# Eight one-bank PSUM tiles in one pool, and layer 0's attention in bursts of up to three half key tiles

## The chip, the cores and the metric

The kernel runs on one core of a Trainium2 chip. The metric is device time in microseconds (us) for one execution, which processes eight images. Five engines work side by side, each through its own instruction queue and in the order of that queue: TensorE (PE, with its weight loads listed as PEld), VectorE (DVE), ScalarE (ACT), GpSimd (POOL) and SyncE (SP, which here only issues DMAs).

## The reference

The input is eight images of 32x32 positions with 384 channels, in fp32. Layer 0 is attention with decomposed relative positions, layer 1 a causal attention followed, for a part of the batch, by an FFN with sign-binarized weights and quantized activations. Cut to what matters:

```python
# layer 0, per image: 6 heads of 64, 1024 positions
qkv = gn(x) @ qkv_w + qkv_b                     # gn: group norm, 32 groups
attn = (q * SCALE) @ k.T
attn += rel_h[:, :, :, :, None] + rel_w[:, :, :, None, :]   # q against row and column tables
x = x + softmax(attn) @ v @ proj_w + proj_b
# layer 1, per image: one head of 384, causal
t = ln(x); t = x + softmax(mask((t @ Wq) @ (t @ Wk).T * scale)) @ (t @ Wv)
# FFN: groups of the batch, NUM_GROUPS = 5, group size 8 // 5 = 1
h = quant(ln(t) @ sign(W1 - mean).T + b1)       # quant: scale by the group's absmax, clip
out = quant(gelu(h) @ sign(W2 - mean).T + b2)   # images beyond the five groups get zero
x = t + out
```

With eight images and five groups of one image each, only images 0 to 4 have an FFN, and its absmax runs over one image.

## The kernel before

The program goes through the images one after the other. For each image b it does the following, and PE's part of each is given with its line.

1. Query, key and value projections of layer 0. `queries_keys(m)` for m = 0, 1, 2 gives the queries of three head pairs (L368, through `project_T`), for m = 3, 4, 5 the keys (L435). After m = 1, 2, 3, `positions(p)` multiplies the queries by the position tables (L461), copies the result from PSUM into pages on ACT (L466) and DVE (L467), and sends it through DRAM (L473, L478) so that it comes back in the layout of scores. `place` splits it in a high and a low part (ACT L491, DVE L492) and puts it into the four tiles `r` by DMA (L499, half of them on SP's queue and half on POOL's). The values come last (L511).
2. Layer 0's attention (`attend0_fast`). For each of three head pairs p, eight key tiles c and two query halves, `scores` makes a half key tile for two heads: two products of queries and keys (L562) and two that add the positions from `r` by a 0/1 matrix (L566). These use row tiles of 64 of PE's rows, so that two heads run side by side. ACT then exponentiates both heads' scores in one instruction of 128x1024 (L571). `values` adds the exponentials up on DVE (L578) and multiplies by the values (L582), in column tiles of 64 columns. The loop makes the two halves of tile c, then the values of tile c - 1. At the first tile of the first pair, `residual` loads x and adds the projection's bias on POOL in one instruction (L545). For image 0 the same loop also calls `binarize` (L255, L256), which computes the FFN's signs on DVE.
3. Output projection (L671, L378), layer norm (`layer_norm_T`: statistics L340, root on ACT L344, normalized rows `xn` on DVE L357, transposes on PE L295, copies L350 and L351), queries of layer 1 (L741), values (L378), the statistics of the next image's group norm (L317, L324), causal attention (L781, L795).
4. For images 0 to 4 the FFN: a second layer norm in both halves, product y1 (L890) with its bias on ACT (L894) and absmax on DVE (L901), the absmax over all partitions (`absmax_scale`: DVE L851, POOL L853, DVE L854 to L857), two gelus of each part on ACT (L914, L915), product y2 (L929), a second absmax, a clip on POOL (L939) and the addition to x on DVE (L943). This last addition and the output DMA (L973) of image b are done within step 1 of image b + 1.

The order of the instructions on each engine is settled when the program is built: instructions are placed by the scheduler of the language's tile framework, and a tile of a pool takes over a buffer from an earlier tile of the same pool in the order in which the code asks for them. PSUM, of eight banks, is divided in two pools:

```python
self.ps_s = pool("ps_s", 2, space=PSUM)   # tiles of two banks: s_tile
self.ps_o = pool("ps_o", 4, space=PSUM)   # tiles of one bank: o_tile
```

`ps_s` holds layer 0's scores, layer 1's scores, the query projections (L368), the third pair's positions and the first output projections. `ps_o` holds all else: key and value projections, the other positions, accumulators, transposes, y1 and y2. In SBUF, `page` has 12 buffers of 128x1024, and `work` has two buffers for `xn`.

Of the kernel before, what the change touches and what calls it, by code (L numbers as in the profile page):

```python
# [9 lines left out]
F32 = mybir.dt.float32  # L10
# [22 lines left out]
MASKED = -3.0e38  # L33

# [4 lines left out]
class Pools:  # L39
    def __init__(self, ctx, tc, path):  # L40
        self.path, self.fast = path, path == "f"

        def pool(name, bufs, **kw):
            return ctx.enter_context(tc.tile_pool(name=f"{path}_{name}", bufs=bufs, **kw))

        self.image_ = pool("image", 11)
        self.page_ = pool("page", 12 if self.fast else 8)
        self.work = pool("work", 2)
        self.small = pool("small", 3)
        self.ps_s = pool("ps_s", 2, space=PSUM)  # L50
        self.ps_o = pool("ps_o", 4, space=PSUM)

    def s_tile(self, name):
        return self.ps_s.tile([P, 2, 512], F32, tag="s", name=f"{self.path}_{name}")
# [20 lines left out]
def conv_attn_hybrid(  # L75
# [42 lines left out]
    def load_weights(pools):  # L118

        nc.scalar.dma_start(out=bqk, in_=qkv_b[0 : 2 * C].rearrange("(m p) -> p m", p=P))  # L120
        nc.vector.memset(rel, 0.0)
        for half in range(2):
            nc.scalar.dma_start(out=rel[half * HD : (half + 1) * HD, 0, : 2 * H - 1], in_=rel_hT)
            nc.scalar.dma_start(out=rel[half * HD : (half + 1) * HD, 1, : 2 * W - 1], in_=rel_wT)
        nc.scalar.dma_start(out=bv, in_=qkv_b[2 * C : 3 * C].rearrange("(m p) -> p m", p=P))
        nc.scalar.dma_start(out=b1_sb, in_=b1.rearrange("(m p) -> p m", p=P))
        src = qkv_w.rearrange("(p k) o -> p k o", k=NC)
        for i in range(3):
            nc.sync.dma_start(out=wqkv_sb[:, :, ts(i, C)], in_=src[:, :, ts(i, C)])
        nc.sync.dma_start(out=wproj_sb, in_=proj_w.rearrange("(k p) o -> p k o", p=P))  # L130
        nc.sync.dma_start(out=pb, in_=proj_b.partition_broadcast(P))
        nc.sync.dma_start(out=wv_sb, in_=wv.rearrange("(k p) o -> p k o", p=P))
        nc.sync.dma_start(out=b2_sb, in_=b2.partition_broadcast(P))

        nc.scalar.mul(wqkv_sb[:, :, 0:C], wqkv_sb[:, :, 0:C], qscale)
        nc.scalar.mul(bqk[:, 0:NPAIR], bqk[:, 0:NPAIR], qscale)
        nc.scalar.mul(rel, rel, 1.0 / qscale)

# [77 lines left out]
    def binarize(pools):  # L216
# [30 lines left out]
        for which, w, dst, n_out, last in pieces("sign"):  # L247
            gs = n_out // NG
            step = min(C // gs, w.shape[1])
            for k in range(0, w.shape[1], step):  # L250
                for g in range(NG):
                    wg, m = w[:, k : min(k + step, w.shape[1]), ts(g, gs)], mean[:, which, g : g + 1]
                    above = pools.work.tile([P, C], F32, tag="xn", name=f"above_{which}_{n_out}")
# [34 lines left out]
    def stages(pools):  # L288
# [17 lines left out]
        def group_norm_T(b, xT=None):  # L306

            xT = load_T(b) if xT is None else xT
            st = pools.small.tile([P, NC, 2, 6], F32, tag="gst", name=f"gst_{b}")
# [24 lines left out]
        def layer_norm_T(xt, xT, half, name, xlo=None):  # L334
# [20 lines left out]
            for i, j in enumerate(js):  # L355
                xn = pools.work.tile([P, C], F32, tag="xn", name=f"xn_{name}_{j}")
# [5 lines left out]

        def project_T(w, cols, xT, name):

            ps = pools.s_tile(name)
            for k in range(NC):
                for half in range(2):
                    nc.tensor.matmul(  # L368
                        ps[:, half, :], w[:, k, cols], xT[:, k, ts(half, 512)],
                        start=(k == 0), stop=(k == NC - 1),  # L370
                    )
            return ps.rearrange("p a n -> p (a n)")
# [19 lines left out]
        def softmax_numerator(sc, n, total, name):  # L392

            nmax = pools.small.tile([P, 1], F32, tag="nmax", name=f"nmax_{name}")
            nc.vector.tensor_reduce(nmax, sc[:, :n], AX.X, ALU.max, negate=True)
            pr = pools.page(f"pr_{name}")
            nc.scalar.activation(pr[:, :n], sc[:, :n], AF.Exp, bias=nmax, accum_out=total)
            return pr
# [15 lines left out]
        def layer0(b, xT):  # L414
# [9 lines left out]
            def queries_keys(m):  # L424
                p = m % NPAIR
                bias = bqk[:, m : m + 1]
                both = project_T(wqkv_sb, ts(m, P), xT, f"qk_{b}_{m}") if m < NPAIR else None
                for half in range(2):
                    t = ts(half, 512)
                    if m < NPAIR:  # L430
                        dst, ps = q[:, p, t], both[:, t]
                    else:
                        ps = pools.o_tile(f"qk_{b}_{m}_{half}")
                        for i in range(NC):
                            nc.tensor.matmul(  # L435
                                ps, wqkv_sb[:, i, ts(m, P)], xT[:, i, t], start=(i == 0), stop=(i == NC - 1)
                            )
# [11 lines left out]
            def positions(p):  # L449
# [6 lines left out]
                for half in range(2):  # L456
                    ps = [pools.o_tile(f"rel_{b}_{p}_{half}_{par}") for par in range(2)] if p < NPAIR - 1 else (
                        pools.s_tile(f"rel_{b}_{p}_{half}").rearrange("i a n -> a i n")
                    )
# [83 lines left out]
            def residual():  # L543
                xt = load_x(pools, b)
                nc.gpsimd.tensor_tensor(xt, xt, pb.unsqueeze(1).to_broadcast([P, NJ, C]), ALU.add)  # L545
# [4 lines left out]
        def attend0_fast(residual, b, q, k, r, v, later):  # L550
# [7 lines left out]
            def scores(p, c, half):  # L558

                sc = pools.s_tile(f"s0_{b}_{p}_{c}_{half}")  # L560
                for par in range(2):
                    nc.tensor.matmul(  # L562
                        sc[:, par, :], k[rows[par], p, ts(c, P)], q[rows[par], p, ts(half, 512)], start=True, stop=False
                    )
                for par in range(2):
                    nc.tensor.matmul(  # L566
                        sc[:, par, :], unit[rows[par], c // 2 % 2].rearrange("i h w -> i (h w)"),
# [3 lines left out]
                last_exp[0] = nc.scalar.activation(pr, sc.rearrange("p a n -> p (a n)"), AF.Exp).ins  # L571
                return pr

            def values(p, c, prs, first, sums, avs):
                if c:
                    for half in range(2):
                        prev = first[half] if c == 1 else sums[half]
                        nc.vector.tensor_tensor(sums[half], prev, prs[half], ALU.add)  # L578
                for half in range(2):
                    for par in range(2):  # L580
                        h = 2 * p + par
                        nc.tensor.matmul(  # L582
                            avs[half][ts(par, HD), :], v[:, c, ts(h, HD)], prs[half][:, ts(par, 512)],
                            start=(c == 0), stop=(c == NJ - 1),
                        )

            def reciprocals(p, tot):

                rt = pools.small.tile([P, 32], F32, tag="rt0", name=f"rt0_{b}_{p}")
# [8 lines left out]
            def set_aside(p, sums, avs):  # L598
# [3 lines left out]
                few = pools.small.tile([P, 2, 2, 16], F32, tag="few", name=f"few_{b}_{p}")  # L602
# [34 lines left out]
            pending = []  # L637
            for p in range(NPAIR):
                sums = [pools.page(f"sum0_{b}_{p}_{half}") for half in range(2)]
                for c in range(NJ):  # L640
                    prs = [scores(p, c, half) for half in range(2)]
                    if c == 0:
                        first = prs
                    if pending:
                        values(*pending.pop())
                    if c == 0:
# [5 lines left out]
                    if b == 0 and xt is None and (c % 2 or p == NPAIR - 1) and next(signs[0]):  # L652
                        xt = residual()
                    if p == 0 and c > 0:
                        with tc.issue_after(last_exp[0]):
                            next(later, None)
                    if c == 3 and p > 0:
                        divide(p - 1, few)
                    pending.append((p, c, prs, first, sums, avs))
                last = (sums, avs)  # L660
            values(*pending.pop())
# [4 lines left out]
            for j in range(4):  # L666
                if j % 2 == 0:
                    both = pools.s_tile(f"pj_{b}_{j}")
                begun.append(both[:, j % 2, :C])
# [13 lines left out]
        def attend0_general(residual, b, q, k, r, v, later):  # L683
# [3 lines left out]
            def scores(u):  # L687
# [4 lines left out]
                sc = pools.s_tile(f"s0_{b}_{j}_{h}")  # L692
                rows = ts(par, HD)
                for half in range(2):
                    nc.tensor.matmul(
                        sc[:, half, :], q[rows, p, ts(j, P)], k[rows, p, ts(half, 512)], start=True, stop=False
                    )
                    for i in range(4):
                        nc.tensor.matmul(
                            sc[:, half, ts(i, P)], r[2 * half + i % 2][rows, p, ts(j, P)],  # L700
# [3 lines left out]
                    sc.rearrange("p a n -> p (a n)"), T, state["tot", j][:, h : h + 1], f"0_{b}_{j}_{h}"  # L704
# [65 lines left out]
        def attend1_fast(xt, b, q, xT, v):  # L770
# [5 lines left out]
            def scores(c):  # L776
                sc = pools.s_tile(f"s1_{b}_{c}")
                for half in range(c // 4, 2):
                    lo = max(0, c * P - half * 512)
                    for k in range(NC):  # L780
                        nc.tensor.matmul(  # L781
                            sc[:, half, lo:], xT[:, c // 4, k, ts(c % 4, P)], q[:, half, k, lo:],
                            start=(k == 0), stop=(k == NC - 1),
                        )
                sc = sc.rearrange("p a n -> p (a n)")
                nc.vector.tensor_tensor(sc[:, ts(c, P)], sc[:, ts(c, P)], maskT, ALU.add)  # L786
                at = sum(NJ - i for i in range(0 if c < 3 else 3, c)) * P
                pr = room[c >= 3][:, at : at + (NJ - c) * P]
                nc.scalar.activation(pr, sc[:, c * P :], AF.Exp)  # L789
# [26 lines left out]
        def attend1_general(xt, b, q, xT, v):  # L816
# [3 lines left out]
            def scores(j):  # L820
                n = (j + 1) * P
                sc = pools.s_tile(f"s1_{b}_{j}")
                for half in range((n + 511) // 512):
                    w = min(512, n - half * 512)
                    for k in range(NC):
                        nc.tensor.matmul(
                            sc[:, half, :w], q[:, j // 4, k, ts(j % 4, P)], xT[:, half, k, :w],
                            start=(k == 0), stop=(k == NC - 1),
                        )
                sc = sc.rearrange("p a n -> p (a n)")  # L830
                nc.vector.tensor_tensor(sc[:, ts(j, P)], sc[:, ts(j, P)], mask, ALU.add)
# [197 lines left out]
```

## Time and profile before

| | us |
|---|---|
| time, median of 3 runs | 2480.84 (2468.26 to 2485.35) |
| the profiled run | 2481.89, span 2480.1, mean granted TensorE clock 0.993 |
| PE busy | 2405.8 |
| DVE busy | 1430.6 |
| ACT busy | 992.7 |
| POOL busy | 231.9 |

The page of the profile lists instructions by source line, with the busy time of the group, the mean time of one, and how long the engine was idle just ahead of them. One image with an FFN takes about 331 us. Layer 0's attention takes about 101 us of an image (for image 6, from 2012.9 to 2113.9). Ends of matmuls are modelled in the profile and neighbouring ones overlap, so times on PE are best read from start to start.

### The profile page before, as it was taken

The page shows a single profiled execution, that of the slowest core. Times are in us where ns is not written, and L with a number is a line of the kernel's source. Part 1 is how long each engine was busy: PE and PEld are TensorE (multiplying, and loading weights), DVE is VectorE, ACT ScalarE, POOL GpSimd, SP SyncE. Part 2 cuts the span into 40 slices and gives each one's busy share as a digit, 9 for nine tenths or more (in the row PEclk, how much of TensorE's full clock was granted, in tenths as well). Part 3 has the DMA queues.
Part 4 walks back from the last instruction along what each step waited for, and adds up shares of the span by engine and source line. Part 5 has one row for each costly group of instructions (what it writes and reads, how often), then busy time and mean ns, then how long its engine had stood idle before and what let it go on. Part 6 is the DMA issues. An engine that isn't in the chain of part 4 may idle for free.

```text
span 2480.1 us, 25259 instructions
## 1 busy us (share of the span) xinstructions
PE 2405.8 (97%) x9378; PEld 1264.7 (51%) x9378; DVE 1430.6 (58%) x2182; ACT 992.7 (40%) x1323; POOL 231.9 (9%) x333
## 2 busy tenths in 40 slices
PE   7989999999999999999999999999999999999998
PEld 3435684345763356743558434566435543554344
DVE  3696554963466744658545486346674258524852
ACT  3441273631555414655127363155541155114520
POOL 0210002200013000030000220001300030002000
PEclk9999999999999999999999999999999999999999
DMA  7812207210054101181110621003500270017100
GB/s 158 246 52 102 77 1 161 68 64 31 8 103 127 51 13 38 28 189 40 39 38 1 161 68 64 8 31 86 143 26 1 68 156 32 1 43 158 30 0 27
DMA packets 154787, 169.92 MB, mean 69 GB/s; under 512 B 113408, under 2 KB 126048, under 8 KB 153120
## 3 DMA queue, kind: packets, MB, share of 16 engines
q1 hardware_dynamic: 134416, 98.93, 16.9%
q0 software_dynamic: 17184, 69.22, 9.2%
q8 instruction: 76, 1.25, 0.2%
q10 hardware_dynamic: 3056, 0.08, 0.1%
q14 instruction: 55, 0.45, 0.1%
HBM read 75.38 MB, written 42.47 MB: 48 GB/s over the span
## 4 chain that ended last, share of the span: by engine, by line
PE 93%; DVE 3%; ACT 2%; issue 1%; DMA 1%; POOL 0%; ACTq 0%; DVEq 0%; POOLq 0%
PE f_s L562 14%; PE f_av L582 14%; PE f_s L781 8%; PE f_av L795 8%; PE f_y L890 6%; PE f_y L929 6%; PE f_qk L435 5%; PE f_v L378 5%; PE f_v L511 5%; PE f_q L741 5%; PE f_qk L368 4%; PE f_s L566 3%; PE f_pj L378 3%; PE f_rel L461 2%; PE f_pj L671 2%; PE f_pt L295 1%
## 5 line engine op out<-in xcount | busy, mean ns | idle before, releaser
L571 ACT ACTIVATE f_pr<-f_s 128x1024 f32<-128x1024 f32 x384 | 390.5, 1025 | 380.9 <-PE f_s L566 343.0
L562 PE MATMUL f_s<-f_q,f_k 64*128 64x512 f32 x1536 | 414.2, 618 | 22.7 <-ACT f_pr L571 22.7
L578 DVE TENSOR_TENSOR f_sum<-f_sum,f_pr 128x1024 f32<-128x1024 f32 x288 | 337.6, 1220 | 97.5 <-ACT f_pr L571 97.0
L582 PE MATMUL f_av<-f_pr,f_v 128*64 128x512 f32 x1536 | 370.0, 604 | 0.0
L566 PE MATMUL f_s<-f_r,unit 64*128 64x512 f32 x768 | 297.6, 773 | 0.0
L562 PEld LDWEIGHTS f_s<-f_q,f_k 64*128 64x128 f32 x1536 | 132.1, 186 | 216.1 <-ACT f_pr L571 146.9
L582 PEld LDWEIGHTS f_av<-f_pr,f_v 128*64 128x64 f32 x1536 | 94.0, 136 | 219.3 <-issue 212.6
L781 PE MATMUL f_s<-f_q,f_lnT 128*128 128x512 f32 (+3 forms) x576 | 197.2, 488 | 0.0
L795 PE MATMUL f_av<-f_v,f_pr 128*128 128x385 f32 x576 | 194.5, 486 | 0.0
L492 DVE TENSOR_TENSOR f_far<-f_near,f_far 64x1024 fp32r<-64x1024 f32 x32 | 95.1, 2973 | 99.4 <-ACT f_far L491 85.1
L435 PE MATMUL f_qk<-f_gnT,wqkv_sb 128*128 128x512 f32 x288 | 135.4, 626 | 16.8 <-DVE f_far L467 16.8
L795 PEld LDWEIGHTS f_av<-f_v,f_pr 128*128 128x128 f32 x576 | 108.6, 190 | 78.6 <-issue 11.5
L499 POOL DMA_DIRECT2D f_r<-f_far x192 | 101.8, 532 | 446.8 <-DVE f_far L492 412.6
L781 PEld LDWEIGHTS f_s<-f_q,f_lnT 128*128 128x128 f32 x576 | 101.4, 190 | 73.9 <-issue 50.2
L368 PE MATMUL f_qk<-f_gnT,wqkv_sb 128*128 128x512 f32 x288 | 132.1, 601 | 3.0 <-DVE f_gnT L329 3.0
L894 ACT ACTIVATE f_h<-f_y,b_sb 128x256 f32<-128x256 f32 x240 | 100.8, 472 | 68.1 <-PE f_y L890 68.0
L901 DVE TENSOR_REDUCE am<-f_h 128x1 f32<-128x1024 f32 (+2 forms) x80 | 71.6, 947 | 97.7 <-ACT f_h L894 97.7
L741 PE MATMUL f_q<-f_lnT,wqk 128*128 128x512 f32 x288 | 127.5, 592 | 0.0
L378 PE MATMUL f_v<-wv_sb,f_lnT 128*128 128x384 f32 x384 | 126.5, 486 | 0.0
L511 PE MATMUL f_v<-wqkv_sb,f_gnT 128*128 128x384 f32 x384 | 125.1, 486 | 0.0
L566 PEld LDWEIGHTS f_s<-f_r,unit 64*128 64x128 f32 x768 | 74.2, 187 | 93.5 <-issue 93.5
L789 ACT ACTIVATE f_pr<-f_s 128x1024 f32<-128x1024 f32 (+3 forms) x64 | 41.7, 651 | 199.1 <-DVE f_s L786 199.1
(162 smaller groups left out, 3091.9 us busy)
## 6 DMA issues: line engine op xcount, KB each, us to landing
f_far<-f_far SPq DMA_DIRECT2D x48, 512.0 KB, 3.8
f_r<-f_far POOLq DMA_DIRECT2D x192, 128.0 KB, 3.5
f_r<-f_far SPq DMA_DIRECT2D x192, 128.0 KB, 3.3
f_gnT<-in_xT SPq DMA_DIRECT2D x24, 512.0 KB, 4.8
f_x<-in_x SPq DMA_DIRECT2D x32, 384.0 KB, 5.6
out_y<-f_x POOLq DMA_DIRECT2D x28, 384.0 KB, 3.8
f_near<-f_far SPq DMA_DIRECT2D x128, 64.0 KB, 4.3
f_w1a<-w1s POOLq DMA_DIRECT2D x5, 1536.0 KB, 6.9
```

Source lines behind the costliest of these rows:

```text
L368: nc.tensor.matmul(ps[:, half, :], w[:, k, cols], xT[:, k, ts(half, 512)], start=(k == 0), stop=(k == NC - 1),)
L378: nc.tensor.matmul(ps[:, :C], xT[:, k, ts(j, P)], w[:, k, cols], start=(k == 0), stop=(k == NC - 1))
L435: nc.tensor.matmul(ps, wqkv_sb[:, i, ts(m, P)], xT[:, i, t], start=(i == 0), stop=(i == NC - 1))
L511: nc.tensor.matmul(ps, keys[:, i, j // 2, j % 2], wqkv_sb[:, i, 2 * C :], start=(i == 0), stop=(i == NC - 1))
L562: nc.tensor.matmul(sc[:, par, :], k[rows[par], p, ts(c, P)], q[rows[par], p, ts(half, 512)], start=True, stop=False)
L566: nc.tensor.matmul(sc[:, par, :], unit[rows[par], c // 2 % 2].rearrange("i h w -> i (h w)"), r[2 * (c // 4) + c % 2][rows[par], p, ts(half ...
L571: last_exp[0] = nc.scalar.activation(pr, sc.rearrange("p a n -> p (a n)"), AF.Exp).ins
L578: nc.vector.tensor_tensor(sums[half], prev, prs[half], ALU.add)
L582: nc.tensor.matmul(avs[half][ts(par, HD), :], v[:, c, ts(h, HD)], prs[half][:, ts(par, 512)], start=(c == 0), stop=(c == NJ - 1),)
L741: nc.tensor.matmul(ps, wqk[:, k, ts(m, P)], xT[:, half, k, :], start=(k == 0), stop=(k == NC - 1))
L781: nc.tensor.matmul(sc[:, half, lo:], xT[:, c // 4, k, ts(c % 4, P)], q[:, half, k, lo:], start=(k == 0), stop=(k == NC - 1),)
L795: nc.tensor.matmul(av[:, : C + 1], prs[c][:, ts(j - c, P)], v[:, c, :], start=(c == 0), stop=(c == j))
```

## The change

PSUM becomes one pool, `ps_o`, of eight tiles of one bank. What was one tile of two banks becomes two tiles of one: scores of layer 0 (one per head), scores of layer 1 (one per 512 keys), query projections, positions, output projections. Instructions on them are divided likewise, so that an exp of 128x1024 becomes two of 128x512.

Layer 0's attention no longer alternates two half tiles of scores with the values of the tile before. The sixteen half tiles of a head pair are made in six bursts of 2, 3, 3, 3, 3 and 2; after each burst's scores come the values of the burst before. `values` works on one half tile. The calls of `residual`, `divide`, `binarize` and `place` follow the bursts.

The bias of the output projection is added to x in eight instructions of 384 columns. `xn` gets a pool of its own with three buffers (some small buffers go from three to two). A square root of a constant, `early_root`, is computed on ACT after the loads of the weights.

```diff
+BURSTS = (2, 3, 3, 3, 3, 2)
+BURSTS_AT = [sum(BURSTS[:i]) for i in range(len(BURSTS))]
...
+        self.xn = pool("xn", 3)
...
-        self.ps_s = pool("ps_s", 2, space=PSUM)
-        self.ps_o = pool("ps_o", 4, space=PSUM)
-
-    def s_tile(self, name):
-        return self.ps_s.tile([P, 2, 512], F32, tag="s", name=f"{self.path}_{name}")
+        self.ps_o = pool("ps_o", 8, space=PSUM)
...
+        early = pools.small.tile([P, 1], F32, tag="early", name="early_root")
+        nc.scalar.activation(early, ones[:, 0:1], AF.Sqrt)
...
-                xn = pools.work.tile([P, C], F32, tag="xn", name=f"xn_{name}_{j}")
+                xn = pools.xn.tile([P, C], F32, tag="xn", name=f"xn_{name}_{j}")
...
-                both = project_T(wqkv_sb, ts(m, P), xT, f"qk_{b}_{m}") if m < NPAIR else None
                 for half in range(2):
                     t = ts(half, 512)
+                    ps = pools.o_tile(f"qk_{b}_{m}_{half}")
+                    for i in range(NC):
+                        nc.tensor.matmul(
+                            ps, wqkv_sb[:, i, ts(m, P)], xT[:, i, t], start=(i == 0), stop=(i == NC - 1)
+                        )
...
-                nc.gpsimd.tensor_tensor(xt, xt, pb.unsqueeze(1).to_broadcast([P, NJ, C]), ALU.add)
+                for j in range(NJ):
+                    nc.gpsimd.tensor_tensor(xt[:, j, :], xt[:, j, :], pb, ALU.add)
...
-                sc = pools.s_tile(f"s0_{b}_{p}_{c}_{half}")
+                sc = [pools.o_tile(f"s0_{b}_{p}_{c}_{half}_{par}") for par in range(2)]
...
-                last_exp[0] = nc.scalar.activation(pr, sc.rearrange("p a n -> p (a n)"), AF.Exp).ins
+                for par in range(2):
+                    last_exp[0] = nc.scalar.activation(pr[:, ts(par, 512)], sc[par], AF.Exp).ins
...
-            pending = []
+            units = [(c, half) for c in range(NJ) for half in range(2)]
+            bursts = [units[at : at + n] for at, n in zip(BURSTS_AT, BURSTS)]
+            pending, first = [], [None, None]
             for p in range(NPAIR):
                 sums = [pools.page(f"sum0_{b}_{p}_{half}") for half in range(2)]
-                for c in range(NJ):
-                    prs = [scores(p, c, half) for half in range(2)]
-                    if c == 0:
-                        first = prs
-                    if pending:
-                        values(*pending.pop())
-                    if c == 0:
+                for n, burst in enumerate(bursts):
+                    prs = [scores(p, *u) for u in burst]
+                    for u in pending:
+                        values(*u)
+                    if n == 0:
...
-                    if b == 0 and xt is None and (c % 2 or p == NPAIR - 1) and next(signs[0]):
+                    if b == 0 and xt is None and next(signs[0]):
                         xt = residual()
-                    if p == 0 and c > 0:
+                    if p == 0 and n > 0:
                         with tc.issue_after(last_exp[0]):
                             next(later, None)
-                    if c == 3 and p > 0:
+                    if n == 2 and p > 0:
                         divide(p - 1, few)
-                    pending.append((p, c, prs, first, sums, avs))
+                    pending = [(p, *u, pr, sums, avs) for u, pr in zip(burst, prs)]
...
-                if j % 2 == 0:
-                    both = pools.s_tile(f"pj_{b}_{j}")
-                begun.append(both[:, j % 2, :C])
+                begun.append(pools.o_tile(f"pj_{b}_{j}")[:, :C])
...
                 for half in range(c // 4, 2):
+                    sc = pools.o_tile(f"s1_{b}_{c}_{half}")
```

## The prediction

> **What bounds the kernel now.** I read the page first: busy shares, then the chain that ended last.
>
> ```profile
> PE 2405.8 (97%) x9378; PEld 1264.7 (51%) x9378; DVE 1430.6 (58%) x2182; ACT 992.7 (40%) x1323; POOL 231.9 (9%) x333
> ...
> PE 93%; DVE 3%; ACT 2%; issue 1%; DMA 1%; POOL 0%; ACTq 0%; DVEq 0%; POOLq 0%
> ...
> L571 ACT ACTIVATE f_pr<-f_s 128x1024 f32<-128x1024 f32 x384 | 390.5, 1025 | 380.9 <-PE f_s L566 343.0
> ```
>
> TensorE (PE) is busy for 97% and carries 93% of the chain, so an edit pays only where PE loses time. I therefore added up, over all pairs of neighbouring PE records, what their start spacing has beyond its steady value: 160 of 2480 us. An fp32 matmul is two records (passes), 0.429 us apart at 512 columns; a pair of 64-row tiles shares a pass slot.
>
> The timeline of one stretch of layer 0's attention shows the steady cycle (start, length, engine, line).
>
> ```profile
> 2039.65 1.13 PE L562 MATMUL f_s<-f_q,f_k 64*128 64x512 f32 x4
> ...
> 2042.03 1.94 PE L582 MATMUL f_av<-f_pr,f_v 128*64 128x512 f32 x8
> 2043.89 1.13 PE L562 MATMUL f_s<-f_q,f_k 64*128 64x512 f32 x4
> ```
>
> A cycle of two half tiles takes 4.25 us (2043.89 to 2048.14 is the next). Scores take 2 x (2 x 0.429 + 0.234 for L566), values 4 x 0.429, together 3.9: PE loses 0.151 us from row-tiled scores to column-tiled values and 0.201 us back. The rest of the 160 us is in waits. In the timeline after the first FFN:
>
> ```profile
> 385.42 5.74 POOL L939 TENSOR_SCALAR f_y<-f_y,qu,ql 128x384 f32<-128x384 f32 x8 [7.15 <-PE f_rel L461]
> 386.10 1.02 DVE L943 SCALAR_TENSOR_TENSOR f_x<-f_y,qs,f_x 128x384 f32<-128x384 f32 x1 [1.75 <-POOL f_y L939]
> 387.16 1.91 DVE L467 COPY f_far<-f_rel 64x512 f32<-64x512 f32 x3
> 387.90 7.05 PE L435 MATMUL f_qk<-f_gnT,wqkv_sb 128*128 128x512 f32 x12 [3.15 <-DVE f_far L467]
> ```
>
> PE waits for a PSUM bank that VectorE (DVE) frees (L467), and DVE waits for GpSimd (POOL). Two more stretches show PE not waiting where it could: between the transposes of the second layer norm, and while the absmax between the FFN's products y1 and y2 goes DVE, POOL, DVE, ACT.
>
> ```profile
> 626.42 0.82 PE L295 MATMUL f_pt<-ident,xn 128*128 128x128 f32 x6
> ...
> 627.08 2.74 PE L368 MATMUL f_qk<-f_gnT,wqkv_sb 128*128 128x512 f32 x6
> ...
> 630.31 3.60 PE L368 MATMUL f_qk<-f_gnT,wqkv_sb 128*128 128x512 f32 x8
> ...
> 631.06 1.28 ACT L344 ACT_TABLE_LOAD   x1
> ...
> 634.40 1.02 PE L368 MATMUL f_qk<-f_gnT,wqkv_sb 128*128 128x512 f32 x2
> ...
> 635.83 0.48 PE L890 MATMUL f_y<-f_lnT,f_w1a 128*128 128x512 f32 x1
> ```
> ```profile
> 669.28 3.59 PE L368 MATMUL f_qk<-f_gnT,wqkv_sb 128*128 128x512 f32 x8
> ...
> 671.10 0.17 DVE L851 TENSOR_REDUCE qg<-am 128x1 f32<-128x16 f32 x1
> ...
> 672.46 0.61 ACT L914 ACTIVATE f_hi<-f_h,qs 128x384 fp32r<-128x384 f32 x1 [2.15 <-DVE qs L857]
> ...
> 673.13 0.79 PE L929 MATMUL f_y<-f_w2a,f_hi 128*128 128x384 f32 x3 [0.26 <-ACT f_hi L914]
> ```
>
> L368 there is the next image's query projection: 16 + 8 passes, 6.87 + 3.43 us of useful work in holes. It can be there because its PSUM tiles come from `ps_s`, which the FFN doesn't use.
>
> [...] L492 took 8.44 us beside the 6.73 us residual add L545. [...] Roughly: after spacing losses of 3.83 to 4.06 us passes took 0.425 us more for a while (1.1 to 2.6 us in all); after 3.14 and 3.15 us none did.
>
> **The change part by part.** The order of instructions in the two built programs was compared engine by engine.
>
> *Bursts.* Eighteen bursts replace 24 in each image. Counted in the programs, row-to-column changes fall from 182 to 136, column-to-row from 175 to 128: 46 x 0.151 + 47 x 0.201 = **-16.4 us**. They fit in the banks: six for three half tiles, two for the accumulators. The exp L571 becomes two of 128x512; nearest row is the ACT copy of that shape, 0.58 us. A cycle of three half tiles is 3 x 1.092 + 6 x 0.429 + 0.352 = 6.2 us of PE, six exps 3.5 us of ACT; the last ends about 3.28 + 1.16 = 4.4 us into the cycle, before PE needs the banks again: nothing, hidden beside PE. The DVE sums keep their number and size; `divide` and `place` come at other bursts, with r's DMAs landing over 10 us before their use.
>
> *Bank waits before the third projection.* With eight banks in rotation L435 takes others than L467 is freeing, and in the new DVE order most L943 come before these copies. The five stalls are 3.94, 3.15, 3.14, 4.06 and 3.83 us; less a 0.2 us mode change each, 17.1; the slow passes behind them 5.8; three other images lose 0.6 each: 17.1 + 5.8 + 1.8 = **-24.7 us**.
>
> *Attention start.* PE waits twice, 1.15 us each (18.4 us over eight images), for an exp. The new order puts four score pairs first (all eight banks), then waits for exp 0's two halves, and again later. From 0 to -18.4; the halves come some 0.3 us earlier at each: **-5 us**.
>
> *Residual add.* Eight POOL instructions of 384 columns (nearest L939, 0.7 us) for one of 6.75. PE hides it, except in image 0, [...] (two L256 took 7.4 us) and PE loses 8.88 us at 145. Binarizing is also called at every burst. Between 0 and -8.9: **-4.5 us**.
>
> *Norm buffers.* The first layer norm loses 1.45 us per image (11.6) on DVE's xn. A third buffer frees only the wait on the transposes, not DVE's own 0.43 us per tile: 0 to -8, taken **-3 us**. The square-root table is loaded (1.28 us, ACT at 13.46) before it is needed: **-1.3 us**.
>
> *What the single pool takes away.* In the new PE order the next image's first query projections stand after the last y2: 24 transposes, 144 y1, 192 y2 in one piece. Tiles of one pool take banks in the order of the code, so the projection can't overtake.
> Absmax: the chain is unchanged, the 3.43 us of work leave it: 5 x 3.43 = **+17.2 us** (15 to 18).
> Second layer norm: before, y1 began 9.41 us after the last attention product, 6.87 of it projection: 2.54 net. After, by DVE's new order: x7's update done at 1.3 us, three low parts (0.51 each) 2.8, fourth xn 3.2, statistics (0.56 + 0.18 + 0.17) 4.2. ACT's fourth cast ends at 4.4, then table load 1.28 and root: 5.9; reciprocal 6.2; four xn with a buffer wait 7.9; transposes, y1 at 8.55. Loss 6.0 x 5 images with an FFN = **+30 us** (25 to 33).
> One matmul (0.86) inside y2, where ACT paces PE anyway: 0 to 4.3, **+2 us**.
> gvar now follows gmean directly; two L781 passes stood between. At the start that wait was 0.96 us: 7 x 0.86 = **+6 us** (0 to 7).
> Clock: the absmax pause becomes 3.6 us, near the point where passes slow: 0 to 25, **+4 us**.
>
> Sum: gains 16.4 + 24.7 + 5 + 4.5 + 3 + 1.3 = 54.9; losses 17.2 + 30 + 2 + 6 + 4 = 59.2; net +4.3 on the profiled 2481.9: **2486 us**. That run is within 0.05% of the median 2480.84 (runs 2468.26 to 2485.35).
>
> **The rivals.**
> A, the sum as above, 2468 to 2504: 0.50. Within it a variant: r arrives late. Image 6, whose order resembles the new one, needed r part 0 44.4 us after its first L461 and had it after 37.4; image 1 took 42.5. Two us late on five images would give 2496.
> B, slower: the clock. If the 3.6 us pause after y1 and the two of 2.2 and 3.0 us in the layer norm lower it, y1 and y2 each begin with up to 2.6 us of slow passes: 5 x (2.6 + 2.6) less the 4 taken is +22: 2508. It decides once the pause passes what separates 3.15 (no slow pass) from 3.83 (slow). For: 3.6 is nearer the latter. Against: y2's start is paced by ACT (a gelu pair each 1.2 us for 0.5 us of matmul), which hides some. 0.28.
> C, faster: the waits collapse together. Attention starts lose nothing (-13.4 more), image 0's stall goes (-4.4), the first norm gains 8 (-5), the second norm costs 25 (-5), y2 and clock nothing (-6): -33.8, 2452. For: all are waits on a buffer or engine that the change relieves. Against: exp's own time stands. 0.22.
> That the bursts aren't made is excluded by the built order.
>
> **How the numbers follow.** About 1% is what a measurement of this kernel tells from no change: faster is below 2456, slower above 2506. The chances are those of C, A and B. The range runs from inside C to beyond B's point, 2455 to 2514, since the clock, image 0 and the attention start each reach some 5 to 20 us.
>
> **What would show it.** Right: three-unit cycles of about 6.2 us; no stall before L435; L943 off PE's way; PE idle about 3.6 us between y1 and y2 and some 5 us in the second layer norm, five times; the first y1 about 8.5 us after the last attention product; no query projection inside the FFN. Wrong: y1 starting within 5 us, attention cycles with exp waits, PE waiting for r at the first L566, or passes of 0.85 us after the pauses.

## The result, and the profile after

The changed kernel takes 2511.5 us (median; 2508.5 to 2514.4) against 2476.8 us for the kernel before in the same rounds (2468.3 to 2485.4): a ratio of 1.014, 95% interval 1.0099 to 1.0181. It is 1.4% slower. That lies inside the stated range, but it is the side to which 0.28 was given, not the likeliest case. The traced run before was 5 us slower than this median, the traced run after 3 us faster than its own, so the traces differ by 26.4 us and the medians by 34.7; in which stage the other 8 us lie, no trace shows.

The page of the changed kernel, with the lines that answer to those of before and one new group:

```profile
PE 2405.9 (96%) x9378; PEld 1296.8 (52%) x9378; DVE 1416.6 (57%) x2182; ACT 1016.2 (41%) x1742; POOL 300.4 (12%) x389
...
PE 93%; DVE 2%; DMA 2%; ACT 1%; POOL 1%; issue 1%; SPq 0%; ACTq 0%; DVEq 0%
...
L569 ACT ACTIVATE f_pr<-f_s 128x512 f32<-128x512 f32 x768 | 408.5, 597 | 351.5 <-PE f_s L563 294.3
...
L542 POOL TENSOR_TENSOR f_x<-f_x,pb 128x384 f32<-128x384 f32 x64 | 117.9, 1871 | 10.0 <-issue 9.7
```

PE's busy time is the same to 0.1 us while the span grew by 26.4 us, so the loss shows as PE's waiting. (Inside the busy time two things offset each other: fewer mode changes, that is, changes between row-tiled and column-tiled products, and the slow passes that are met below.) ACT pays 18 us for halving the exps, and nobody waits for that. POOL's residual add L542 takes 1.87 us for one of eight; the single instruction before took 6.75.

Both traces can be cut at PE's first instruction of each stage. Summed over the images, the stages differ as follows (after minus before, us of the profiled runs):

| stage of PE | difference |
|---|---|
| start to the first position product | -1.1 |
| first position product to the values (L457 to L507) | -20.6 |
| values and layer 0's attention | -8.3 |
| output projection and first layer norm | -6.1 |
| layer 1's queries to the end of its attention | +9.5 |
| end of attention to the next first position product: second norm, y1, y2, and now all of the moved projections | +53.5 |

Five times 0.86 us of projection went from the last stage to the second one, so the FFN's own loss is 57.8 and the second stage's own gain 24.9. The sum is 26.9, the rest of 0.5 lies at the end.

The second layer norm in the timeline after (image 1):

```profile
630.21 1.15 PE L296 MATMUL f_pt<-ident,xn 128*128 128x128 f32 x9
...
633.42 0.52 PE L296 MATMUL f_pt<-ident,xn 128*128 128x128 f32 x3 [2.06 <-DVE xn L358]
...
634.47 1.28 ACT L345 ACT_TABLE_LOAD   x1
...
636.22 1.26 DVE L358 TENSOR_SCALAR xn<-f_x,lmv,lrs 128x384 f32<-128x384 f32 x3
...
636.75 2.82 PE L296 MATMUL f_pt<-ident,xn 128*128 128x128 f32 x12 [2.81 <-DVE xn L358]
...
639.22 0.71 PE L890 MATMUL f_y<-f_lnT,f_w1a 128*128 128x512 f32 x1
```

PE stands idle for 2.06 and 2.81 us where the projection used to be. The last twelve transposes take 2.82 us where six took 0.82: their starts are 0.21 us apart, not 0.108. The clock is low there: the trace has a granted clock of 0.50 from 636.75 to 639.20, and 1.00 over the same stage before (626 to 636). The low clock reaches into y1: in the five images its first passes, one to eight of them, start 0.27 to 0.57 us apart in place of 0.23 (0.32 for the very first), 3.6 us more than before in all. Between y1 and y2 the bracket gives the pause and its releaser, and the projection follows only after y2:

```profile
672.76 0.40 PE L890 MATMUL f_y<-f_lnlo,f_wrest 128*128 128x512 f32 x1
676.83 0.97 PE L929 MATMUL f_y<-f_w2a,f_hi 128*128 128x384 f32 x3 [3.67 <-ACT f_hi L914]
677.98 1.33 PE L929 MATMUL f_y<-f_w2a,f_hi 128*128 128x384 f32 x3 [0.19 <-ACT f_hi L914]
```
```profile
712.08 10.46 PE L430 MATMUL f_qk<-f_gnT,wqkv_sb 128*128 128x512 f32 x24
722.47 1.99 PE L457 MATMUL f_rel<-f_q,rel 64*128 64x512 f32 x8
```

From the fifth pass of y2 on, seven starts lie 0.32 us apart where most lay 0.17 to 0.18 apart before. The clock records say the same: 0.50 from 677.3 to 680.7.

In layer 0's attention the bursts run as they were meant to, from 2060.78 to 2066.98 in 6.2 us (PE, image 6), but pair 1 meets a new wait:

```profile
2060.78 1.13 PE L559 MATMUL f_s<-f_q,f_k 64*128 64x512 f32 x4
...
2064.26 2.79 PE L580 MATMUL f_av<-f_pr,f_v 128*64 128x512 f32 x12
2066.98 1.13 PE L559 MATMUL f_s<-f_q,f_k 64*128 64x512 f32 x4
...
2074.29 0.50 PE L563 MATMUL f_s<-f_r,unit 64*128 64x512 f32 x2 [1.08 <-DMA f_r<-f_far]
```

The wait stands at the same place in images 1 to 7; only here does the profile name its releaser.

What holds that transfer shows in POOL's queue at the same time, where six additions stand ahead of the remaining issues for `r`:

```profile
2056.51 0.55 POOL L495 DMA_DIRECT2D f_r<-f_far  x1
2057.08 11.79 POOL L542 TENSOR_TENSOR f_x<-f_x,pb 128x384 f32<-128x384 f32 x6
2068.81 3.17 POOL L495 DMA_DIRECT2D f_r<-f_far  x6
```

### The profile page after: what moved, and what is told of

It is laid out like the page before. It is cut to its first block, busy times and chain, and to the rows that moved or that the text cites. A ratio compares the mean times of both kernels' runs of the same rounds, so it can differ in the third digit from the quotient of the medians.

```text
span 2506.5 us, 25716 instructions
## 1 busy us (share of the span) xinstructions
PE 2405.9 (96%) x9378; PEld 1296.8 (52%) x9378; DVE 1416.6 (57%) x2182; ACT 1016.2 (41%) x1742; POOL 300.4 (12%) x389
## 4 chain that ended last, share of the span: by engine, by line
PE 93%; DVE 2%; DMA 2%; ACT 1%; POOL 1%; issue 1%; SPq 0%; ACTq 0%; DVEq 0%
PE f_s L559 14%; PE f_av L580 14%; PE f_qk L430 10%; PE f_av L794 7%; PE f_s L781 7%; PE f_y L929 7%; PE f_y L890 7%; PE f_v L368 5%; PE f_q L739 5%; PE f_v L507 4%; PE f_s L563 4%; PE f_pj L368 2%; PE f_rel L457 2%; PE f_pj L669 2%; PE f_pt L296 1%; PE f_pj L674 1%
## 5 line engine op out<-in xcount | busy, mean ns | idle before, releaser
L569 ACT ACTIVATE f_pr<-f_s 128x512 f32<-128x512 f32 x768 | 408.5, 597 | 351.5 <-PE f_s L563 294.3
L559 PE MATMUL f_s<-f_q,f_k 64*128 64x512 f32 x1536 | 412.6, 608 | 6.3 <-ACT f_pr L569 6.3
L577 DVE TENSOR_TENSOR f_sum<-f_sum,f_pr 128x1024 f32<-128x1024 f32 x288 | 373.6, 1347 | 17.5 <-ACT f_pr L569 17.0
L580 PE MATMUL f_av<-f_pr,f_v 128*64 128x512 f32 x1536 | 359.6, 601 | 0.0
L563 PE MATMUL f_s<-f_r,unit 64*128 64x512 f32 x768 | 305.8, 767 | 7.8 <-issue 6.7
L430 PE MATMUL f_qk<-f_gnT,wqkv_sb 128*128 128x512 f32 x576 | 256.9, 600 | 2.0 <-DVE f_gnT L330 2.0
L559 PEld LDWEIGHTS f_s<-f_q,f_k 64*128 64x128 f32 x1536 | 145.6, 186 | 173.7 <-issue 98.7
L430 PEld LDWEIGHTS f_qk<-f_gnT,wqkv_sb 128*128 128x128 f32 x576 | 108.1, 191 | 144.2 <-issue 131.4
L794 PEld LDWEIGHTS f_av<-f_v,f_pr 128*128 128x128 f32 x576 | 108.7, 190 | 78.5 <-issue 11.5
L788 ACT ACTIVATE f_pr<-f_s 128x512 f32<-128x512 f32 (+3 forms) x96 | 47.1, 490 | 208.8 <-DVE f_s L786 154.3
L507 PE MATMUL f_v<-wqkv_sb,f_gnT 128*128 128x384 f32 x384 | 125.1, 486 | 0.0
L542 POOL TENSOR_TENSOR f_x<-f_x,pb 128x384 f32<-128x384 f32 x64 | 117.9, 1871 | 10.0 <-issue 9.7
```

What stands on the lines that cost most here:

```text
L430: nc.tensor.matmul(ps, wqkv_sb[:, i, ts(m, P)], xT[:, i, t], start=(i == 0), stop=(i == NC - 1))
L507: nc.tensor.matmul(ps, keys[:, i, j // 2, j % 2], wqkv_sb[:, i, 2 * C :], start=(i == 0), stop=(i == NC - 1))
L559: nc.tensor.matmul(sc[par], k[rows[par], p, ts(c, P)], q[rows[par], p, ts(half, 512)], start=True, stop=False)
L563: nc.tensor.matmul(sc[par], unit[rows[par], c // 2 % 2].rearrange("i h w -> i (h w)"), r[2 * (c // 4) + c % 2][rows[par], p, ts(half, 512) ...
L569: last_exp[0] = nc.scalar.activation(pr[:, ts(par, 512)], sc[par], AF.Exp).ins
L577: nc.vector.tensor_tensor(sums[half], prev, pr, ALU.add)
```

## The experiments

The theory after the result, called F: the single pool puts the query projections behind the FFN, which costs more than everything else gains. Its rivals: the bursts cost (R), or the projections filled time that was hidden anyway (P). Times are medians; "before" is 2476.4 to 2477.9 us in these rounds. Stages are read as in the table above.

**Bursts alone.** The kernel before with its two pools; only layer 0's loop changes.

```diff
-            def scores(p, c, half):
+            def scores(p, c, half, third=False):
...
+                if third:
+                    sc = [pools.o_tile(f"s0_{b}_{p}_{c}_{half}_{par}") for par in range(2)]
...
+                    prs = [scores(p, *u, third=(i == 2)) for i, u in enumerate(burst)]
```

> The kernel before with bursts alone: the two pools stay, the third half tile of a burst takes two one-bank tiles of ps_o (its exp in two halves), everything else as before. Theory F (the single pool costs the query projections their place inside the FFN, and that is what makes the change slower): the projections stay in the FFN, the mode changes fall as in the change, so 16 us less than before, about 2461 us (2455 to 2468), and the FFN of an image takes its 82 to 83 us from the last attention product to the first position product. Rival R (bursts bring nothing, because exps, r or the sums take the time back in new waits): 2475 or more.

2464.4 us, ratio 0.9946 (0.9927 to 0.9965). The attention of every image from the second on is 2.1 us shorter, 16.7 us with image 0, against 16.4 worked out; the FFN stands as before. (The medians differ by 12.6 us: in this trace the start is 1.6 us longer and the waits ahead of the values 1.5.) R is out: without the pool change the bursts give what the mode changes cost.

**The pool without bursts.** The changed kernel with

```diff
-BURSTS = (2, 3, 3, 3, 3, 2)
+BURSTS = (2,) * 8
...
-                    if b == 0 and xt is None and next(signs[0]):
+                    if b == 0 and xt is None and (n % 2 or p == NPAIR - 1) and next(signs[0]):
...
-                    if n == 2 and p > 0:
+                    if n == 3 and p > 0:
```

> The changed kernel with bursts of two half tiles each, so that scores and values alternate as before; the calls of binarize and divide are put back to where the kernel before has them; the pool of eight banks and all else stay. Theory F: 16 us of mode changes come back, all else stays, about 2526 us (2518 to 2534). Rival R (bursts are what costs, in waits for r or exps): at or below the changed kernel's 2511.

2523.2 us, ratio 1.0186 (1.0167 to 1.0205), 12 us above the changed kernel. Images 1 to 7 take the attention time of before within 0.14 us, and the wait for `r` in pair 1 isn't there; image 0 is 7.7 us longer than with bursts. So bursts help inside the new pool as well, though in images 1 to 7 by only 0.5 to 0.9 us each: the new wait takes the other 1.2 to 1.5. F's "all else stays" was not quite right.

**The projections alone moved.** The kernel before with

```diff
-            ps = pools.s_tile(name)
+            ps = [pools.o_tile(f"{name}_{half}") for half in range(2)]
...
-                        ps[:, half, :], w[:, k, cols], xT[:, k, ts(half, 512)],
+                        ps[half], w[:, k, cols], xT[:, k, ts(half, 512)],
```

> The kernel before with one edit: the query projections take two one-bank tiles of ps_o in place of one two-bank tile of ps_s. Theory F: they leave the FFN, which then takes some 93 to 95 us from the last attention product to the first position product and gives up 57 us over five images; the stalls ahead of the third projection, 23 us, may go with it, because the position copies then come after most of the additions L943. So 2500 to 2535, likely 2513. Rival P (the projections fill time that would be hidden anyway): within 8 us of before.

2547.1 us, ratio 1.0274 (1.025 to 1.0298). Two tiles in another pool cost 70 us. The stretch from the end of attention to the next position product grows by 63 us, 67 with the one product that left it: P is out. That the loss is larger than in the changed kernel (57.8) doesn't make the filler worth more: with two `xn` buffers, which this kernel has, the changed kernel loses 65 us in the same count (run with two norm buffers, below). The stalls ahead of the third projection did not go with it (the second stage grew by 6.4 us, of it 4.3 the moved product), so the later position products alone don't remove them; in the changed kernel they went with the pool of eight.

**The residual add in one piece.** The changed kernel with

```diff
-                for j in range(NJ):
-                    nc.gpsimd.tensor_tensor(xt[:, j, :], xt[:, j, :], pb, ALU.add)
+                nc.gpsimd.tensor_tensor(xt, xt, pb.unsqueeze(1).to_broadcast([P, NJ, C]), ALU.add)
```

> The changed kernel with the bias added by one GpSimd instruction, as before. Theory Q (in the changed kernel PE waits 1.2 to 1.5 us at the second score unit of pair 1 in seven images, because GpSimd issues the second half of r's transfers behind eight additions that take 1.87 us each beside VectorE's sums): these waits go, 9 us less in images 1 to 7, about 2503; [...]. Rival S (r is late because its chain begins later or its transfers collide): the waits stay, 2511.

2500.7 us, ratio to the kernel before 1.0094 (1.0075 to 1.0113): 11 us better than the changed kernel. POOL in its trace:

```profile
2050.38 6.72 POOL L541 TENSOR_TENSOR f_x<-f_x,pb 128x3072 f32<-128x3072 f32 x1
2060.98 2.13 POOL L495 DMA_DIRECT2D f_r<-f_far  x4 [3.88 <-DVE f_far L488]
```

POOL is through with the addition some 12 us earlier and now waits for DVE's part of r (3.88 us), where that part waited for POOL. The attention of images 1 to 7 is 2.1 us shorter than before, and no wait for `r` is left. Theory Q holds. Image 0 lost 0.35 us.

**Keys from the other pool.** The kernel before with

```diff
-                both = project_T(wqkv_sb, ts(m, P), xT, f"qk_{b}_{m}") if m < NPAIR else None
+                both = project_T(wqkv_sb, ts(m, P), xT, f"qk_{b}_{m}") if m <= NPAIR else None
```

> The kernel before with one edit: the third projection of an image (the first one of the keys) takes its PSUM from the two-bank pool ps_s, not from the banks that the position copies hold. Theory W (the stalls of 3.1 to 4.1 us ahead of it, with the slow passes behind them, are waits for those banks and nothing else): images 1 to 5 take 27.5 to 29 us from the first position product to the values in place of 28.9 to 32.2, 12 to 20 us in all, about 2460. Rival V (VectorE's queue is late in any case, so that the next instruction waits as long): within 5 us of before.

2496.1 us, ratio 1.0073 (1.0048 to 1.0098): slower. The stall only moved to the next product, the third pair's positions, which also use `ps_s`:

```profile
384.34 1.13 PE L461 MATMUL f_rel<-f_q,rel 64*128 64x512 f32 x4
389.70 1.53 PE L461 MATMUL f_rel<-f_q,rel 64*128 64x512 f32 x4 [4.24 <-DVE f_k L441]
```

There PE waits 4.24 us for a key copy in the same DVE queue. The choice of bank alone doesn't settle it; this left open whether the copies or what stands ahead of them is late.

**Additions behind the copies.** The kernel before with

```diff
-                    unfinished.pop()()
+                    with tc.issue_after(copied[1]):
+                        unfinished.pop()()
```

where `copied[1]` is the second pair's last position copy L467.

> The kernel before with one edit: the eight additions L943 of the last image are put behind the second pair's position copies on VectorE; pools and PSUM tiles as before. Theory W2 (the stall ahead of the third projection is a PSUM bank whose copy stands behind additions that wait for GpSimd; whoever takes the bank from these copies waits as long, as the run with the keys in ps_s showed): images 1 to 5 take about 27.5 us from the first position product to the values in place of 28.9 to 32.2, 15 to 19 us in all, about 2460. Rival V2 (VectorE or ACT are late with the copies themselves): less than 6 us gained.

2455.0 us, ratio 0.9907 (0.9877 to 0.9936).

```profile
378.47 5.42 PE L435 MATMUL f_qk<-f_gnT,wqkv_sb 128*128 128x512 f32 x12 [0.53 <-DVE f_far L467]
```

The bracket falls from 3.15 to 0.53 us and the slow passes behind it are gone (7.05 to 5.42 us for the same twelve). Images 1 to 5 take 20.0 us less up to the values. W2 holds: the stall was DVE's queue, blocked by an addition that waited for POOL. The rest of the difference between the traces, 6.4 us, is in image 0's attention, which the edit doesn't touch. There PE waits 8.09 us at 144 in the trace before, 2.35 us at 138 in this one, and 1.04 at 139 in the trace with the keys from the other pool, whose edit doesn't touch it either; that kernel's six runs fall in two groups, 2486 to 2488 and 2495 to 2499 us. So the stall may well differ from run to run, and a gain or loss of under 8 us in image 0 isn't told by one trace.

**Products later.** The changed kernel waits 10.09 us in image 0, ahead of the attention, for weights:

```profile
81.59 8.61 PE L286 MATMUL f_wqk<-f_wqkT 128*128 128x384 f32 x18 [10.09 <-DMA f_wqkT<-in_wkT]
```

```diff
                 join_biases(pools)
-                multiply_out(pools)
...
+                    if b == 0 and p == 1 and n == 3:
+                        multiply_out(pools)
```

> The changed kernel with one call moved: the product of layer 1's query and key weights is asked for in the second pair of image 0's attention, not ahead of the attention. Theory D (in the changed kernel PE waits 10.7 us at 72 for these weights' transfer, then runs slow passes for 2 us, because the built order has the product ahead of the attention): image 0 gets 10 to 13 us shorter, about 2499. Rival E (image 0 waits for VectorE's sign computation in any case, so that the time comes back there): 2508 or more.

2519.2 us, 8 us worse than the changed kernel. That wait is gone, but PE waits in two other places for DVE, which computes the signs in this image:

```profile
127.97 0.31 PE L611 MATMUL f_den<-few,fold 128*64 128x32 f32 x4 [4.32 <-DVE few L603]
...
140.33 1.19 PE L558 MATMUL f_s<-f_q,f_k 64*128 64x512 f32 x1 [7.14 <-DVE seen L409]
```

From the values to the end of its attention image 0 takes 9 us longer than in the changed kernel, and the two waits are 11.5 us. Rival E was right.

**Two norm buffers.** The changed kernel with

```diff
-        self.xn = pool("xn", 3)
+        self.xn = pool("xn", 2)
```

> The changed kernel with two xn buffers in place of three. If the third buffer is what shortens the way from the end of layer 0's attention to layer 1's queries by 0.77 us per image, that goes back to 20.7 us (8 images, 6 us), and the second layer norm gets longer by up to 1 us in five images. If the pool of eight banks does it, both stay.

2520.6 us in one run. The stage from layer 0's attention to layer 1's queries stays 0.77 us shorter, so the third buffer doesn't do that; it is as short in the run of the pool without bursts, and unchanged with bursts alone in two pools. But the second layer norm is 1.2 us longer in five images and the stage after the queries 0.4 us in eight: 9 us that the third buffer gives, by this one run.

**PE kept busy in the pause.** The changed kernel with

```diff
+            idle = pools.o_tile(f"idle_{b}")
+            for i in range(5):
+                nc.tensor.matmul(idle[:, :C], wqk[:, 0, :P], wqk[:, 1, :], start=True, stop=True)
             s, _ = absmax_scale(am.rearrange("p i n -> p (i n)"), f"1_{b}")
```

> The changed kernel with five products of constants added between y1 and y2, whose result nothing reads; they take about 3.2 us of the pause in which the absmax is found. Theory C (the pause also lowers PE's clock, and y2's first passes are slow by that): the first passes of y2 come 0.17 us apart in place of 0.32, and y1's start to y2's end gets 0.5 to 1.5 us shorter per image, 2.5 to 7 us in all. Rival N (y2's start is paced by ACT's gelus alone): no shorter.

2507.3 us in one run; y1 and y2 of the five images together are 4.4 us shorter.

```profile
674.14 3.39 PE L906 MATMUL f_idle<-wqk 128*128 128x384 f32 x10
677.97 0.79 PE L932 MATMUL f_y<-f_w2a,f_hi 128*128 128x384 f32 x3 [0.45 <-ACT f_hi L917]
679.13 0.79 PE L932 MATMUL f_y<-f_w2a,f_hi 128*128 128x384 f32 x3 [0.36 <-ACT f_hi L917]
679.76 1.41 PE L932 MATMUL f_y<-f_w2a,f_lo 128*128 128x384 f32 x6
```

The three passes at 679.13 take 0.79 us and the next six 1.41, as in the kernel before; in the changed kernel they take 1.33 and 1.94. The mean granted clock of the run is 0.990, against the changed kernel's 0.988. Theory C holds, and it sizes the clock: of the 4.4 us, 3.9 are in y2, 0.8 us per image (0.5 to 1.3); the other 0.5 are in y1, ahead of the added products. Most of a pause's cost is the pause.

**Combinations.** First a kernel of two pools with bursts, the keys from `ps_s`, three `xn` buffers and the early root:

```diff
+            def scores(p, c, half, third=False):
...
+                both = project_T(wqkv_sb, ts(m, P), xT, f"qk_{b}_{m}") if m <= NPAIR else None
...
+        self.xn = pool("xn", 3)
...
+        nc.scalar.activation(early, ones[:, 0:1], AF.Sqrt)
```

> The kernel before with its two pools, and in them: bursts with a third half tile in ps_o, the first key projection from ps_s, three xn buffers, the early square root. The residual add stays one instruction. If the parts add up (bursts 16.7, key banks 12 to 20, norm 6, start 1): about 2440 (2433 to 2450). If they share time, 2450 to 2460.

2468.7 us, ratio 0.9966 (0.9953 to 0.998), above both expectations. Bursts gave 17.9, the norms 6.3 with what they cost elsewhere; the keys took 11.5 back. Then the same with the additions behind the copies in place of the keys:

```diff
-                both = project_T(wqkv_sb, ts(m, P), xT, f"qk_{b}_{m}") if m <= NPAIR else None
+                both = project_T(wqkv_sb, ts(m, P), xT, f"qk_{b}_{m}") if m < NPAIR else None
...
-                    unfinished.pop()()
+                    with tc.issue_after(copied[1]):
+                        unfinished.pop()()
```

> The kernel before with its two pools, and in them bursts with a third half tile in ps_o, the additions L943 behind the second pair's copies, three xn buffers, the early square root; the residual add is one instruction. If the parts add up as measured one by one (bursts 16.7, additions 15 to 19, norms 6, start 1): about 2437 (2432 to 2445). If the additions' gain isn't there: 2452 or more.

2436.5 us (2435.8 to 2439.5), ratio 0.9833 (0.9808 to 0.9859).

```profile
PE 2381.8 (98%) x9378; PEld 1271.6 (52%) x9378; DVE 1427.6 (59%) x2182; ACT 992.6 (41%) x1420; POOL 243.8 (10%) x333
```

The parts add up: 19.2 us ahead of the values, 19.6 in the attention, 6.3 in the norms. This beats the changed kernel by 75 us and the kernel before by 41.

## Why the prediction was right or wrong

The sum of 2486 us was 25 too low. The measured time falls where rival B was put (2508), but mostly not by B's mechanism: B asked for 26 us of slow passes, and about 13 came, 9 more than the sum had taken. That the number lies inside the range owes something to luck: what the working missed in the attention (17.6 us on the traces) was about as large as what B would have added. Point by point, with what was predicted, then measured:

- *Bursts, -16.4.* Right: -16.7 alone. That the halved exps are hidden was right too (ACT +18 us, no wait for it in a burst).
- *Bank waits, -24.7.* Right: -24.9. That DVE's queue behind POOL is the cause in the kernel before was shown by moving the additions.
- *What the single pool takes away.* Absmax +17.2 and y2 +2: measured 20.8 and 4.6. The pause itself is as worked out; the 3.6 above 17.2 are the slow first passes of y1, and of y2's 4.6 the run with PE kept busy gives 3.9 to the clock. Second layer norm +30: measured 32.3, y1 starting 9.0 us after the attention, counted as in the working, where 8.55 was worked out. The slow transposes, 11 x 0.1 us, which the working left out, are more than that difference, so the rest of the chain was a little shorter than thought. The mechanism was right and its sum close: with the 4 for the clock the working had 53.2, the FFN lost 57.8. But about 13 of the 57.8 are the clock, and the rest 4.4 less than the 49.2 worked out for it.
- *Residual add, -4.5.* The step that failed. It said "PE hides it" and priced an addition at 0.7 us after L939. In the trace before, half of the 40 L939 ran beside DVE's copies L467 (0.81 us there, 0.65 for the others); the additions, 48 of 64 beside the sums L577, take 1.87 us each, all eight 14.7. What its queue holds up was not priced: POOL also issues half of r's transfers, and "r's DMAs landing over 10 us before their use" took only pair 0's slack. Pair 1 waits 1.2 to 1.5 us in seven images, 9.4 us, and the run with the add in one piece takes these waits away. The variant under rival A had r late too, but for pair 0 and from its own chain, in five images by two us. Only what the pieces free for DVE in image 0 was counted, not what eight of them cost: the trace gives 14.7 us for eight pieces beside 6.75 for one. DVE slows as well: five sums L577 beside these pieces take 9.65 us, 1.93 each, where one without them takes 1.22. By what mechanism, no run shows.
- *Attention start, -5.* Wrong in size: nothing. PE still waits twice, 0.45 us each by the bracket, and behind each wait the two heads' passes no longer start in pairs 0.006 us apart: in image 6 the four of L559 start at 2043.08, 2043.57, 2043.62 and 2044.10 (three and one in the lines below). Each head's bank has a half exp of its own in this kernel; whether that is the cause was not shown.

```profile
2043.08 1.18 PE L559 MATMUL f_s<-f_q,f_k 64*128 64x512 f32 x3 [0.45 <-ACT f_pr L569]
2043.64 0.79 PE L563 MATMUL f_s<-f_r,unit 64*128 64x512 f32 x1
2044.10 0.59 PE L559 MATMUL f_s<-f_q,f_k 64*128 64x512 f32 x1
```

  With the residual in one piece the attention gains 2.1 us per image, which is what the mode changes alone give, so nothing is left for the start.
- *Image 0.* The 8.88 us at 145 went, and a wait of 10.1 us for weights at 72 came, which the built order shows and the working didn't look at. Image 0's attention gained 3.3 us where 7 were counted, but the stall before may itself differ from run to run, as said above.
- *Norm buffers, -3.* Measured -6.1 in the first norm, of which the third buffer is not the cause. The single pool is what is left, since the gain is there with two buffers, without bursts and with the residual in one piece, and absent with bursts alone in two pools; by which of its tiles, no run tells. (In two pools a third buffer gives 3.7 there.) *gvar, +6*: 9.5; the wait is 1.2 us by the trace, not the 0.96 taken from the start of the kernel. *Early root, -1.3*: the start came 1.1 us earlier, but it moves by up to 1.6 us between kernels that don't touch it, so this isn't told.
- *Clock, +4.* Too small. The granted clock was 0.50 behind the pauses of the layer norm and of the absmax in all five images, as B said. B's price was 5 x 5.2; measured are 3.6 at the start of y1, 3.9 at the start of y2 and up to 5 x 1.1 in the transposes, about 13 together. The dividing line was also drawn with a wrong measure: the losses of 3.83 to 4.06 us contain the first slow pass. As idle time in the trace before, the stalls with slow passes behind them (granted clock 0.50) are 3.04, 3.15 and 3.27 us, those without (1.00) 2.87 and 2.88, so the 3.67 us after y1 lay well on the slow side.

Counted against the sum of +4.3: the stages of the profiled runs give 26.9, which is 22.6 more. The attention (r's late transfer, its start, image 0) makes 17.6 of it, the FFN 4.6, gvar 3.5, less 3.1 in the first norm.

## What to carry to other kernels

A pool is also an order: work that has a buffer of its own can fill another stage's holes, and merging pools takes that away even when the banks suffice, so compare the order of the merged program stage by stage before counting what the banks free. Here eight pieces of an addition took 14.7 us where one instruction took 6.75, and the transfers queued behind them on the same engine came later: PE lost 1.2 to 1.5 us on them in each of seven images; price a piece from a stretch with the same neighbours. A stall shown as a wait for a buffer may be a queue behind the release: moving what stands ahead of the release was worth 20 us, while taking a bank of the other pool only moved the wait to the next product.

## What the hardware showed that was not expected

GpSimd's addition of 128x3072 takes 6.75 us in one piece and 14.7 us in eight, and VectorE's sums beside the eight take 1.93 us each in place of 1.22. In each of five images, after two pauses of 2.06 and 2.81 us with three transposes between them, the transposes that followed came 0.21 us apart in place of 0.108 (granted clock 0.50), although in the kernel before single stalls of 2.87 and 2.88 us were not followed by slow passes (granted clock 1.00); stalls of 3.04, 3.15 and 3.27 us were (0.50).
